# Layer 2 attention: position sums in 128x32 column tiles, and one score tile in three squared on ScalarE

## The chip, the cores and the metric

The kernel runs on one core of a Trainium2 chip. A core has engines that run side by side, each with a queue of its own: TensorE (PE in the profile, its weight loads PEld), VectorE (DVE), ScalarE (ACT), GpSimd (POOL) and SyncE (SP, which only issues DMAs here). They tell each other through semaphores when a tile is ready or free. Matmul results go to PSUM[...]; all other tiles lie in SBUF. The metric is the device time of one execution in microseconds, the median of the runs.

## The reference

The whole computation is a four-layer network over x of shape (2, 64, 64, 128) in fp32. Only the attention of layer 2 is touched. There the input is layer-normed, taken as 2 batches of L = 4096 tokens of 128 channels with 4 heads of 32, and this is computed:

```
q, k, v = silu(x @ Wq + bq), silu(x @ Wk + bk), silu(x @ Wv + bv)
u = x @ Wu + bu
rel = pos_w[S - 1 + m - n]                     # a Toeplitz matrix; a table index too large is held at the end
pos_attn = einsum('nm,bmd->bnd', rel, v)
scores = (qh @ kh) / sqrt(32)                  # per head
scores = where(m <= n, scores * scores, 0)
self_attn = silu(scores) @ vh
a = layernorm(concat(self_attn, pos_attn)) * ln_gamma + ln_beta
out = relu(u * a @ Wf + bf) + x
```

So every score is multiplied by a scale, squared, masked causally and put through SiLU before it weighs the values; there is no softmax. The position part is a product of a table of lags with the values, independent of the scores.

## The kernel before

The stages run one after another (layer 0, layer 1, layer 2's attention and FFN, layer 3's). A second copy of the program follows behind a condition and is not executed with these inputs. `layer2_attn` works on blocks of 512 queries: 16 blocks (b, qb), in the order qb = 7, 0, 6, 1, 5, 2, 4, 3 for each batch. A block loops over its 4qb + 4 key chunks of 128, the last four of which are on the diagonal and get narrower (512, 384, 256, 128 queries). 288 chunks are worked in all. For each chunk, `scores(i, k)` computes two PSUM tiles `l2sc` of 128x1024, each with two heads (L1273: four matmuls with 32 rows of contraction, on four row groups of the array). PSUM holds two such tiles, so the next chunk's tile can only be written when the tile of the same place has been read.

The two tiles are then taken out of PSUM and squared into SBUF tiles `l2es` (seven of them), in two different ways. The first tile of each chunk is squared by ScalarE in one instruction, with the scale in it (L1282); on the diagonal VectorE then multiplies its first 128 columns by the causal mask (L1295). The second tile is scaled by VectorE (L1290, and on the diagonal L1286 for the masked 128 columns) and then squared in SBUF by GpSimd (L1297). `silu()` applies SiLU on ScalarE to both tiles of the chunk before (L1303), and `values()` multiplies those of two chunks before with the values, four matmuls of 128x32 weights into four partition groups of one PSUM bank `l2av` (L1316).

Beside this run the jobs of a hand-written planner: generators that issue a piece of their work at each `yield`. After each chunk, as many pieces are taken from the head of the list as the sum of all pieces divided by the chunks left. The jobs are the keys and values of a group of tokens (`keys`), their suffix sums (`suffixes`), the queries of the next block (`prepare`), the position sums (`positions`), and, when a block's chunks are done, `join` (transposition, layer norm, three POOL products L1217 to L1219) and `output` (projection and addition to x). `join` finishes the rest of its block's position sums at once.

`positions` sums the Toeplitz products of a block of 512 queries. The table `toe` holds for each lag d = 0 to 31 a 128x128 block. For each of the four query chunks n of a block, one matmul for each k up to n adds `toe` block n - k times value chunk k (L1178: 128x128 weights, 128 columns moving); all later keys have one and the same table entry, so one product of a suffix sum with the matrix `late` adds them (L1189). The sums of four chunks lie in one PSUM bank `l2pos`, which VectorE copies out (L1199).

The order on each engine's queue is not that of the code: a scheduler sets it when the program is built. For an even stretch of the loop it is, on ScalarE, the square of a chunk, the SiLU of its first tile, the SiLU of its second tile (which waits for GpSimd), then the next chunk; on TensorE the scores of chunk k, the values of chunk k - 2, and a piece of the position sums.

Of the kernel before, what the change touches and what calls it, by code (L numbers as in the profile page):

```python
# [9 lines left out]
AF = mybir.ActivationFunctionType  # L10
ALU = mybir.AluOpType
# [3 lines left out]
P = 128  # L15
# [3 lines left out]
NC = L // P  # L19
# [19 lines left out]
class Net:  # L39
# [928 lines left out]
    def layer2_attn(self):  # L968
# [3 lines left out]
        nc, tc, ins = self.nc, self.tc, self.ins  # L972
        pos_w = ins["L2_attn_pos_rev"]
        with ExitStack() as st:
# [7 lines left out]
                out=flip,  # L982
# [7 lines left out]
            toe = wp.tile([P, L], F32, tag="toe", name="toe")  # L990
            with tc.tile_pool(name="l2r", bufs=1) as rp:
                rev = rp.tile([P, L], F32, tag="rev", name="rev")
                nc.sync.dma_start(
                    out=rev,
# [51 lines left out]
            def finish(key):  # L1046
                while key in jobs:
                    piece(key)
# [120 lines left out]
            def positions(b, qb, i):  # L1169
                finish(("suf", b))  # L1170
                v, suf = vs[b], sufs[b]
                pos = ps.tile([P, 4, C], F32, tag="pos", name=f"l2pos{b}_{qb}", bufs=1)
                done = 0
                for j in range(4):
                    n = 4 * qb + j
                    last = n == NC - 1
                    for k in range(n + 1):
                        nc.tensor.matmul(  # L1178
                            pos[:, j, :],
                            lhsT=toe[:, (n - k) * P : (n - k + 1) * P],  # L1180
                            rhs=v[:, k, :],
                            start=(k == 0),
                            stop=(last and k == n),
                        )
                        done += 1
                        if done % 4 == 0:
                            yield
                    if not last:
                        nc.tensor.matmul(  # L1189
                            pos[:, j, :],  # L1190
                            lhsT=suf[:, 0, n + 1 : n + 2].broadcast_to([P, P]),
                            rhs=late,
                            start=False,
                            stop=True,
                        )
                if i >= 2:
                    finish(("out", i - 2))
                cats[i] = ap.tile([P, 4, 2 * C], F32, tag="cat", name=f"l2a{b}_{qb}")
                nc.vector.tensor_copy(cats[i][:, :, C:], pos)  # L1199
# [52 lines left out]

            root = float(HD) ** -0.5
            raw, squared = [], []

            def scores(i, k):


                b, qb = order[i]
                finish(("keys", b, k // 4))  # L1260
                q, kT = queries[i][0], kTs[b]

                off = max(0, k - 4 * qb) * P
                diag = k >= 4 * qb
                mask = tri.unsqueeze(1).broadcast_to([P, 2, P])
                out = []
                for pair in range(2):
                    t = f"{b}_{qb}_{k}_{pair}"
                    sc = ps.tile([P, 2, 512], F32, tag="sc", name=f"l2sc{t}")
                    for h2 in range(2):  # L1270
                        h = 2 * pair + h2
                        hs = slice(h * HD, (h + 1) * HD)
                        nc.tensor.matmul(  # L1273
                            sc[:, h2, off:],
                            lhsT=kT[hs, k * P : (k + 1) * P],
                            rhs=q[hs, off:],
                            start=True,
                            stop=True,
                        )
                    out.append((sc, ap.tile([P, 2, 512], F32, tag="es", name=f"l2es{t}", bufs=7)))  # L1280
                (sc, es), (sc1, es1) = out
                nc.scalar.activation(es[:, :, off:], sc[:, :, off:], AF.Square, scale=root)  # L1282
                lo = off
                if diag:
                    lo = off + P
                    nc.vector.scalar_tensor_tensor(  # L1286
                        es1[:, :, off:lo], sc1[:, :, off:lo], root, mask, ALU.mult, ALU.mult
                    )
                if lo < 512:
                    nc.vector.tensor_scalar(  # L1290
                        es1[:, :, lo:], sc1[:, :, lo:], root, None, ALU.mult
                    )
                if diag:
                    part = es[:, :, off:lo]
                    nc.vector.tensor_tensor(part, part, mask, ALU.mult)  # L1295
                part = es1[:, :, off:]
                nc.gpsimd.tensor_tensor(part, part, part, ALU.mult)  # L1297
                raw.append((i, k, off, (es, es1)))

            def silu():  # L1300
                i, k, off, es = raw.pop(0)
# [544 lines left out]
```

## Time and profile before

| What | Value |
|---|---|
| Median of 3 runs | 5194.89 us (5192.98 to 5206.92) |
| The profiled execution's own time | 5199.35 us |
| Its span | 5197.4 us |
| Granted TensorE clock, mean | 0.898 |
| Layer 2's attention loop | from about 2150 to 3490 us of the span |
| Position sums L1178, TensorE | 2112 records, mean 293 ns; weight loads mean 199 ns |
| Squares on ScalarE, L1282 | 288, mean 937 ns |
| Evacuations on VectorE, L1290 | 272, mean 1127 ns |
| Squares on GpSimd, L1297 | 288, mean 1751 ns |
| SiLU on ScalarE, L1303 | 576, mean 984 ns |

A matmul in fp32 leaves two records in the trace, so 2112 records are 1056 products. The means mix the wide tiles with the narrow ones of the diagonal. Matmuls on different row or column groups run at the same time, so the time that counts is from the start of one group to the start of the next, not the duration of one record. A line of the waits names who was idle, what released it, the total, how many times, and the longest. The chain of waits is followed back from the last instruction, at each step to whatever released it.

### The profile page before, as it was taken

The numbers are of one execution on the slowest core, as the hardware profiler recorded it, in microseconds if no ns is written. First come the engines' busy times: TensorE is split into PE (matmuls) and PEld (weight loads), VectorE is DVE, ScalarE is ACT, GpSimd is POOL, SyncE is SP. The second block draws the span as 40 slices with busy tenths as digits, with TensorE's granted clock in tenths as the row PEclk, the third lists the DMA queues.
The fourth block names the chain that finished last, engine by engine and source line by source line (L and its number), as shares of the span: only waits on it lengthen the run. The fifth ranks groups of instructions, "written<-read, shape, count | busy, mean of one in ns | idle before, by whom it ended". The sixth has DMA issues, their size and how long they took to land.

```text
span 5197.4 us, 69148 instructions
## 1 busy us (share of the span) xinstructions
PE 4641.6 (89%) x28133; PEld 2278.3 (44%) x28133; DVE 2851.6 (55%) x4850; ACT 2406.8 (46%) x2783; POOL 749.9 (14%) x434
## 2 busy tenths in 40 slices
PE   7999999999999946789889988885999999999776
PEld 6433333443333335444344434443986444444432
DVE  2568776667878888744444344444023333333477
ACT  3556666566666624466666766551003222222200
POOL 1000000000000030244444455440002000000000
PEclk7899999999999968889999999886559999999889
DMA  4222323333233200000000000002320000000000
GB/s 126 65 56 45 60 65 76 84 66 67 51 57 60 44 8 1 24 1 1 1 1 1 1 1 1 1 1 67 122 74 1 0 0 1 0 0 0 5 11 23
DMA packets 132256, 165.10 MB, mean 32 GB/s; under 512 B 13233, under 2 KB 75665, under 8 KB 131025
## 3 DMA queue, kind: packets, MB, share of 16 engines
q1 hardware_dynamic: 110016, 143.38, 12.9%
q10 hardware_dynamic: 21904, 17.12, 1.1%
q8 instruction: 226, 3.70, 0.3%
q14 instruction: 110, 0.89, 0.1%
HBM read 131.10 MB, written 29.36 MB: 31 GB/s over the span
## 4 chain that ended last, share of the span: by engine, by line
PE 73%; DVE 13%; ACT 6%; POOL 5%; issue 2%; DMA 1%; ACTq 0%; DVEq 0%; POOLq 0%; SPq 0%
PE l0sc L593 17%; PE l0o L547 9%; PE scl L1610 8%; PE oTl L1627 8%; PE l2sc L1273 5%; POOL l2es L1297 3%; PE l2pos L1178 3%; PE f3ex L1784 2%; PE l2av L1316 2%; PE f2po L1488 2%; PE f2ph L1462 2%; ACT l2es L1303 2%; DVE l2es L1290 2%; DVE l0acc L615 2%; ACT l2es L1282 2%
## 5 line engine op out<-in xcount | busy, mean ns | idle before, releaser
L615 DVE TENSOR_TENSOR l0acc<-l0acc,l0es 128x1024 f32<-128x1024 f32 x988 | 1209.9, 1225 | 535.6 <-PE l0o L547 370.4
L607 ACT ACTIVATE l0es<-l0sc 128x1024 f32<-128x1024 f32 x992 | 940.3, 1031 | 384.2 <-PE l0sc L593 383.2
L593 PE MATMUL l0sc<-l0mv,ka 64*64 64x512 f32 x8192 | 990.9, 616 | 18.8 <-ACT l0es L607 16.5
L1303 ACT ACTIVATE l2es<-l2es 128x1024 f32<-128x1024 f32 (+3 forms) x576 | 563.5, 984 | 344.0 <-POOL l2es L1297 304.6
L1297 POOL TENSOR_TENSOR l2es<-l2es 128x1024 f32<-128x1024 f32 (+3 forms) x288 | 504.1, 1751 | 671.9 <-DVE l2es L1290 617.5
L1635 DVE TENSOR_TENSOR accl<-accl,esl 128x1024 f32<-128x1024 f32 x240 | 294.1, 1225 | 540.7 <-ACT esl L1621 482.9
L593 PEld LDWEIGHTS l0sc<-l0mv,ka 64*64 64x64 f32 x8192 | 297.6, 136 | 622.8 <-issue 377.2
L1273 PE MATMUL l2sc<-l2q,l2kT 32*128 32x512 f32 (+3 forms) x2304 | 427.6, 642 | 129.6 <-ACT l2es L1282 99.2
L1290 DVE TENSOR_SCALAR l2es<-l2sc 128x1024 f32<-128x1024 f32 (+3 forms) x272 | 306.6, 1127 | 397.9 <-PE l2sc L1273 397.2
L1621 ACT ACTIVATE esl<-scl 128x1024 f32<-128x1024 f32 x240 | 245.5, 1023 | 550.8 <-PE scl L1610 550.8
L547 PE MATMUL l0o<-l0es,l0v 128*32 128x512 f32 x3968 | 495.0, 602 | 0.0
L1610 PE MATMUL scl<-l3qT,l3kT 128*128 128x512 f32 x1024 | 484.0, 595 | 1.8 <-DVE bok_l L247 1.8
L1627 PE MATMUL oTl<-esl,l3v 128*128 128x512 f32 x960 | 448.5, 592 | 0.0
L1178 PEld LDWEIGHTS l2pos<-l2v,toe 128*128 128x128 f32 x2112 | 266.9, 199 | 166.3 <-issue 165.1
L1316 PE MATMUL l2av<-l2es,l2v 128*32 128x512 f32 (+3 forms) x2304 | 317.2, 619 | 2.5 <-ACT l2es L1303 2.5
L1178 PE MATMUL l2pos<-l2v,toe 128*128 128x128 f32 x2112 | 309.3, 293 | 0.0
L1282 ACT ACTIVATE l2es<-l2sc 128x1024 f32<-128x1024 f32 (+3 forms) x288 | 270.0, 937 | 73.0 <-PE l2sc L1273 72.1
L1610 PEld LDWEIGHTS scl<-l3qT,l3kT 128*128 128x128 f32 x1024 | 192.8, 191 | 233.2 <-issue 218.6
L868 POOL TENSOR_TENSOR l1y<-l1y,l1gb 128x1024 f32<-128x1024 f32 x8 | 20.2, 2529 | 1858.5 <-DVE l1y L862 1838.3
L1627 PEld LDWEIGHTS oTl<-esl,l3v 128*128 128x128 f32 x960 | 182.4, 190 | 229.6 <-issue 225.8
L547 PEld LDWEIGHTS l0o<-l0es,l0v 128*32 128x32 f32 x3968 | 106.9, 109 | 337.8 <-issue 337.8
L1273 PEld LDWEIGHTS l2sc<-l2q,l2kT 32*128 32x128 f32 x2304 | 128.0, 195 | 245.9 <-ACT l2es L1282 136.5
(435 smaller groups left out, 4483.0 us busy)
## 6 DMA issues: line engine op xcount, KB each, us to landing
l0mv<-l0qd SPq DMA_DIRECT2D x128, 256.0 KB, 5.8
l0mv<-l0hd SPq DMA_DIRECT2D x256, 128.0 KB, 4.0
l0mv<-l0wd SPq DMA_DIRECT2D x128, 128.0 KB, 6.1
l0wd<-l0rw SPq DMA_DIRECT2D x4, 2048.0 KB, 7.5
l0hd<-l0hst SPq DMA_DIRECT2D x32, 256.0 KB, 2.2
f2w<-in_L_ffn_weight_dram ACTq DMA_DIRECT2D x32, 256.0 KB, 4.2
f2w<-in_L_ffn_weight_dram ACTq DMA_DIRECT2D x8, 1024.0 KB, 4.8
f2w<-in_L_ffn_weight_dram SPq DMA_DIRECT2D x8, 1024.0 KB, 5.1
```

The costliest lines, as they stand in the source:

```text
L547: nc.tensor.matmul(o[0][at : at + HD, :], lhsT=v[:, 2 * j + s, HD * h : HD * (h + 1)], rhs=es[s][:, h, :], start=(j == 0), stop=(j == NX * ...
L593: nc.tensor.matmul(sc[64 * c : 64 * c + 64, h, :], lhsT=ka[rows, k0 : k0 + 64], rhs=mv[rows, yb, :], start=True, stop=True,)
L607: nc.scalar.activation(es, sc, AF.Exp)
L615: nc.vector.tensor_tensor(entry[5], entry[5], es, ALU.add)
L1178: nc.tensor.matmul(pos[:, j, :], lhsT=toe[:, (n - k) * P : (n - k + 1) * P], rhs=v[:, k, :], start=(k == 0), stop=(last and k == n),)
L1273: nc.tensor.matmul(sc[:, h2, off:], lhsT=kT[hs, k * P : (k + 1) * P], rhs=q[hs, off:], start=True, stop=True,)
L1290: nc.vector.tensor_scalar(es1[:, :, lo:], sc1[:, :, lo:], root, None, ALU.mult)
L1297: nc.gpsimd.tensor_tensor(part, part, part, ALU.mult)
L1303: nc.scalar.activation(e[:, :, off:], e[:, :, off:], AF.Silu)
L1316: nc.tensor.matmul(avs[i][hs, off:], lhsT=vs[b][:, k, hs], rhs=es[h // 2][:, h % 2, off:], start=(k == 0), stop=last,)
L1610: nc.tensor.matmul(sc[:, i, :], lhsT=kT[:, k * P : (k + 1) * P], rhs=qs, start=True, stop=True,)
L1627: nc.tensor.matmul(oT, lhsT=v[:, k, :], rhs=es[:, i, :], start=(k == 0), stop=(k == NC - 1),)
```

## The change

Two things are altered, both in layer 2's attention. `positions` now runs over lags d: for each lag it multiplies the table block with all value chunks that it meets in this block of queries, up to four chunks or 512 columns moving at once. The weights are cut in four parts of 128x32 that write four partition groups of the same bank; the suffix products are cut in the same way. A piece of the job is one lag (the lags at the end go together). `scores` no longer has a fixed way for each of the two tiles: a counter runs over all tiles of the stage, and every third tile is squared on ScalarE, the two others go through VectorE and GpSimd. So of three chunks, one has both tiles on VectorE and GpSimd, one has its first tile on ScalarE and one its second. The number of jobs' pieces given to the planner, the buffers and the DMAs stay as they are. In the changed kernel the position matmul is at L1177, the ScalarE square at L1289, the mask product at L1292, the VectorE evacuation at L1301, the GpSimd square at L1304, SiLU at L1310 and the values at L1323.

```diff
--- before.py
+++ after.py
@@ -1170,29 +1170,32 @@
                 finish(("suf", b))
                 v, suf = vs[b], sufs[b]
                 pos = ps.tile([P, 4, C], F32, tag="pos", name=f"l2pos{b}_{qb}", bufs=1)
-                done = 0
+                n0 = 4 * qb
+                for d in range(n0 + 4):
+                    j0 = max(0, d - n0)
+                    for c in range(0, P, 32):
+                        nc.tensor.matmul(
+                            pos[c : c + 32, j0:, :],
+                            lhsT=toe[:, d * P + c : d * P + c + 32],
+                            rhs=v[:, n0 + j0 - d : n0 + 4 - d, :],
+                            start=(d == 0),
+                            stop=False,
+                        )
+                    if d < n0 or j0 == 1:
+                        yield
                 for j in range(4):
-                    n = 4 * qb + j
-                    last = n == NC - 1
-                    for k in range(n + 1):
+                    n = n0 + j
+                    if n == NC - 1:
+                        continue
+                    for c in range(0, P, 32):
                         nc.tensor.matmul(
-                            pos[:, j, :],
-                            lhsT=toe[:, (n - k) * P : (n - k + 1) * P],
-                            rhs=v[:, k, :],
-                            start=(k == 0),
-                            stop=(last and k == n),
-                        )
-                        done += 1
-                        if done % 4 == 0:
-                            yield
-                    if not last:
-                        nc.tensor.matmul(
-                            pos[:, j, :],
-                            lhsT=suf[:, 0, n + 1 : n + 2].broadcast_to([P, P]),
+                            pos[c : c + 32, j, :],
+                            lhsT=suf[:, 0, n + 1 : n + 2].broadcast_to([P, 32]),
                             rhs=late,
                             start=False,
-                            stop=True,
-                        )
+                            stop=(n == min(n0 + 3, NC - 2)),
+                        )
+                yield
                 if i >= 2:
                     finish(("out", i - 2))
                 cats[i] = ap.tile([P, 4, 2 * C], F32, tag="cat", name=f"l2a{b}_{qb}")
@@ -1252,6 +1255,7 @@
 
             root = float(HD) ** -0.5
             raw, squared = [], []
+            turn = [0]
 
             def scores(i, k):
 
@@ -1278,24 +1282,27 @@
                             stop=True,
                         )
                     out.append((sc, ap.tile([P, 2, 512], F32, tag="es", name=f"l2es{t}", bufs=7)))
-                (sc, es), (sc1, es1) = out
-                nc.scalar.activation(es[:, :, off:], sc[:, :, off:], AF.Square, scale=root)
-                lo = off
-                if diag:
-                    lo = off + P
-                    nc.vector.scalar_tensor_tensor(
-                        es1[:, :, off:lo], sc1[:, :, off:lo], root, mask, ALU.mult, ALU.mult
-                    )
-                if lo < 512:
-                    nc.vector.tensor_scalar(
-                        es1[:, :, lo:], sc1[:, :, lo:], root, None, ALU.mult
-                    )
-                if diag:
-                    part = es[:, :, off:lo]
-                    nc.vector.tensor_tensor(part, part, mask, ALU.mult)
-                part = es1[:, :, off:]
-                nc.gpsimd.tensor_tensor(part, part, part, ALU.mult)
-                raw.append((i, k, off, (es, es1)))
+                for sc, es in out:
+                    turn[0] += 1
+                    part = es[:, :, off:]
+                    if turn[0] % 3 == 0:
+                        nc.scalar.activation(part, sc[:, :, off:], AF.Square, scale=root)
+                        if diag:
+                            part = es[:, :, off : off + P]
+                            nc.vector.tensor_tensor(part, part, mask, ALU.mult)
+                        continue
+                    lo = off
+                    if diag:
+                        lo = off + P
+                        nc.vector.scalar_tensor_tensor(
+                            es[:, :, off:lo], sc[:, :, off:lo], root, mask, ALU.mult, ALU.mult
+                        )
+                    if lo < 512:
+                        nc.vector.tensor_scalar(
+                            es[:, :, lo:], sc[:, :, lo:], root, None, ALU.mult
+                        )
+                    nc.gpsimd.tensor_tensor(part, part, part, ALU.mult)
+                raw.append((i, k, off, [es for _, es in out]))
 
             def silu():
                 i, k, off, es = raw.pop(0)
```

## The prediction

> **What bounds the kernel now.** I read the page first, then a table of windows to find the stage, the waits inside it, the chain of waits, and a timeline of an even stretch. The page's span is 5197.4 us. The edit touches one stage, layer 2's attention, and a wholly hidden or wholly exposed edit there can only move these 1340 us (columns after the window: length, then busy time and count of PE, weight loads, DVE, ACT, POOL, then the granted clock):
>
> ```profile
> 2150.00:3490.00 1340.00, 1190.18 (x7806) 585.02 (x7807) 606.33 (x996) 881.18 (x956) 629.54 (x349) 0.92 0.00 1
> 2560.00:2590.00 30.00, 29.50 (x228) 13.38 (x220) 10.96 (x9) 27.60 (x28) 17.03 (x9) 1.00 0.00 1
> ```
>
> TensorE looks full (89%), ScalarE has 66% and POOL 47%. In the even stretch ScalarE is at 92% too, so two engines are nearly full, and shares alone do not say which work to move. The waits of the stage (total us, times, longest):
>
> ```profile
> ACT l2es L1303 <- POOL l2es L1297: 304.6, 199, 8.6
> DVE l2es L1295 <- ACT l2es L1282: 185.5, 59, 8.3
> PE l2sc L1273 <- ACT l2es L1282: 99.2, 89, 7.9
> ```
>
> Each waits on the next: TensorE's scores wait for the ScalarE square that frees a score buffer (L1282), that square stands behind a SiLU (L1303), and the SiLU waits for POOL's square (L1297). The chain of waits (start, us, what) shows one full turn in the even stretch and then the first turn on the diagonal:
>
> ```profile
> 2578.30 1.21 PE l2sc L1273 x8
> ...
> 2579.61 1.23 DVE l2es L1290
> ...
> 2580.91 1.90 POOL l2es L1297
> 2582.84 1.06 ACT l2es L1303
> 2583.89 0.92 ACT l2es L1282
> ...
> 2584.86 1.21 PE l2sc L1273 x8
> ...
> 2590.45 0.92 ACT l2es L1282
> ...
> 2591.40 0.42 DVE l2es L1295
> 2591.82 0.33 DVE l2es L1286
> 2592.15 0.88 DVE l2es L1290
> ...
> 2593.19 1.90 POOL l2es L1297
> 2595.11 1.06 ACT l2es L1303
> ```
>
> Scores, evacuation, POOL square, SiLU, ScalarE square, next scores: 2584.86 - 2578.30 = 6.56 us, and two key chunks pass in it, because the scores of chunk k+1 wait for the square of chunk k, which waits for the POOL square of chunk k-1. So 3.28 us for a chunk. TensorE's own work is just under that (start, us, then line and operation):
>
> ```profile
> 2581.47 1.14 PE L1273 MATMUL l2sc<-l2q,l2kT 32*128 32x512 f32 x8
> 2582.54 1.06 PE L1316 MATMUL l2av<-l2es,l2v 128*32 128x512 f32 x8
> 2583.54 1.16 PE L1178 MATMUL l2pos<-l2v,toe 128*128 128x128 f32 x8
> ...
> 815.77 1.92 PE L547 MATMUL l0o<-l0es,l0v 128*32 128x512 f32 x16
> 817.63 1.12 PE L379 MATMUL l0pk<-l0xT,wqkv 128*128 128x512 f32 x2
> ```
>
> From start to start: scores 1.07, values 1.00, position sums 1.09 (from the 2580.37 group to 2581.47), together 3.16. The last two rows, from layer 0, are 128x32 column tiles, twice as many as a values group: 817.63 - 815.77 = 1.86 us, so a second group in the same tiling costs 0.86 and the first 1.00.
>
> Taking the start of every eighth score matmul in the timelines as a chunk's start, I sorted the 288 chunks: 114 even ones off the diagonal (374.2 us, 3.28 each), 23 of 3.7 to 4.4 us (93.5 us, two position pieces each, TensorE full), 64 diagonal ones (295.0 us), and 87 at the block changes, where output projection, layer norm and left-over position sums run (568.5 us).
>
> **What the Trainium skill says.** PSUM — Partial Sum Buffer, "Engine vs sequencer instructions": the queues of ScalarE, VectorE and GpSimd are strict FIFO, so a waiting instruction holds all behind it. The trace agrees: DVE stood 185.5 us at the mask product (L1295) while L1286 and L1290 behind it had their scores. TensorEngine Tiling (Array Packing), "Key Properties": tiles work in parallel and a change of tiling mode drains the array; agreed, 0.86 against 1.00 us above. GPSIMD Engine Reference, "3.1": a two-input fp32 operation takes about twice VectorE's time; here POOL's 128x1024 square takes 1892 ns, VectorE's evacuation 1223 ns. TensorE: Matmul & The Clock Gate, Part 1: an idle window of about 3.4 us halves the clock; agreed at 2537.03, where after 7.88 us of idling the score group took 2.09 us instead of 1.14.
>
> **The change, part by part.**
>
> *Position sums.* 2112 matmul records of 128x128 (1056 products, two records each) become 2304 of 128x32 by up to 512 columns, the form and shapes of L1316. Four value chunks took 1.09 us alone and 0.92 in a run (28 records and 2 of the suffix from 2463.63 to 2467.08: 0.115 each); now 0.86, since they stand right behind the values group in the same tiling. TensorE gains 0.23 us a chunk where pieces stand alone: even work falls to 1.07 + 1.00 + 0.86 = 2.93. If the tiling switch were still paid, 1.00; if weight loads showed, bounded by the 1.09 of before. The gain counts only where TensorE sets the end. At the block changes, runs of up to some 60 records (7 us) stand on the chain; 6% of that is 0.4 us in 16 blocks: -6 us. The suffix products become four column tiles of 128 columns: same columns, no difference counted.
>
> *Squares.* The tiles now go DVE+POOL, DVE+POOL, ScalarE in turn, so three chunks make a round: c (both tiles by DVE and POOL), a (first tile on ScalarE), b (second on ScalarE). ScalarE loses 96 squares of 0.94 us, DVE and POOL gain 96 each of 1.13 and 1.75. Busy time per round stays below TensorE's 8.8: ScalarE 2 x 1.0 + 6 x 1.06 = 8.4, POOL 4 x 1.89 = 7.6, DVE 4.9. What decides is the order. The built program has on ScalarE, in nearly every even stretch:
>
> ```
> SQ a0, silu a0, silu a1(POOL) | SQ b1, silu b0(POOL), silu b1 | silu c0(POOL), silu c1(POOL) | SQ a0 ...
> ```
>
> So the square of a stands behind the SiLU of c's second tile, which has to wait for two POOL squares in line. With the chain's durations and 0 at the start of c's scores: DVE c0 1.31 to 2.54, c1 to 3.76; POOL c0 2.61 to 4.51, c1 to 6.41; SiLU c1 6.44 to 7.50; square a0 to 8.42; scores of b start at 8.46. Scores of a started between, at 2.93 and, its second pair, at 3.8 (c1 evacuated), so their POOL square ends at 8.31 and delays nothing. From b to the next c TensorE needs 2.93, and the square b1 (behind SiLU a1, 10.5) ends at 11.46. A round is 11.5 us, 3.83 a chunk, where before it was 9.84. The same working gives 6.56 for two chunks of before, which the trace shows. 114 x 0.55 = +62 us. Bounds: not below 2.93 a chunk (-40 us), since TensorE has that work; not above both POOL squares and the slow clock in each round, 13.5 us (+140).
>
> In the 23 chunks with two position pieces the round is 8.46 + (1.07 + 1.00 + 2 x 0.86) = 12.25, 4.08 each against 4.07: 0.
>
> *Diagonal.* Before, the mask product stands on DVE ahead of the evacuation and waits for ScalarE's square, so a turn (square, mask, two evacuations, POOL, SiLU) covers one chunk: about 5.4, 4.3 and 3.3 us as the tiles shrink. Twelve undisturbed diagonals took 16.9 us on average. Now each tile is handled in its own turn, and only an a chunk keeps the mask ahead of the evacuation. With the same durations (POOL 1.89, 1.47, 1.05, 0.63 us by width) I get about 13 us for a diagonal that begins with b, 14.5 with c, 15.8 with a; 6, 2 and 4 of the twelve begin so: 14.2 on average, 12 x -2.7 = -32 us. Bounds: 0, and 10 us each (TensorE's work there), -83.
>
> *Block changes.* POOL has two more squares in six chunks (3.8 us) next to the 7.1 us of L1217 to L1219, ScalarE one or two fewer. In the stall from 2525.89 to 2537.03 the built order lets one square in between those three products, but then three squares follow: nearly even. I take +0.9 us in 16 blocks, +14, with -30 and +50 as ends.
>
> Sum: +62 - 32 + 14 - 6 = +38 us on the profiled execution's 5199.35 (span 5197.4), which lies 4.5 above the runs' median of 5194.89; on the median, 5233. No DMA is moved: SP's order is the same instruction for instruction.
>
> **Rivals.** (1) Faster: the mask wait. If diagonals fall to TensorE's work, about 10.5 us, all sixteen give -100 us against the +70 of the other terms, near 5165. It decides once a diagonal saves over 4.4 us. For it: 185.5 us of DVE waiting at L1295. Against: the POOL and SiLU part of the turn stays. (2) No change, 5195: the block changes gain what I count as cost, because ScalarE's squares there (stalls of up to 7.9 us) come sooner. (3) Slower still: the round leaves TensorE idle for 1.75 us in 11.5, and the clock halves; scores and values then add some 2 us a round, 38 rounds, +75, near 5300. Against: TensorE has 8.8 us of work in a round, and 1.75 us is about half of the idle window that the page names. (4) The column tiles do not overlap and the sums take four times as long, hundreds of us; L1316 has the same form and does overlap (2304 records of 619 ns in 317.2 us), under 1%.
>
> **How the numbers follow.** Forecast 0.58, with 5212 to 5275 as its own range; (1) 0.19; (2) 0.13; (3) with (4) 0.10. About 0.3%, 15.6 us, is what can be told from no change. Slower 0.58 + 0.10 = 0.68, same 0.13, faster 0.19. The range 5170 to 5300 leaves out half of (1) and half of (3).
>
> **What would show it.** Right: even chunks in rounds of 11.5 us with the step of 8.4 us from c to b; SiLU waiting for POOL well above 304.6 us; DVE's wait at the mask product (now L1292) far below 185.5; position groups 0.86 us behind a values group; other stages unchanged. Wrong: even chunks at 3.28 or less (the order on ScalarE then did not hold), diagonals at 11 us, or a granted clock clearly below 0.92 in the stage.

## The result and the profile after

| | Before | After |
|---|---|---|
| Median (four runs each, same chip) | 5199.78 us | 5238.52 us (5237.44 to 5245.0) |
| Ratio to the kernel before | 1 | 1.0077, 95% interval 1.0058 to 1.0095 |
| The profiled execution's own time | 5199.35 us | 5245.0 us |
| Its span | 5197.4 us | 5242.2 us |
| Mean granted TensorE clock | 0.898 | 0.898 |

The kernel is 0.77% slower, 39 us by the medians. (The four runs before are the three of the table ahead of the prediction and a fourth of 5204.68 us.) The table of windows of the changed kernel, for the stage and for an even stretch (window, length, then busy time and count of PE, weight loads, DVE, ACT, POOL, then the granted clock):

```profile
2150.00:3540.00 1390.00, 1186.92 (x8395) 417.98 (x8394) 725.18 (x1106) 783.27 (x865) 795.43 (x445) 0.92 0.00 1
2570.00:2597.00 27.00, 23.58 (x184) 5.96 (x176) 12.36 (x11) 18.75 (x20) 17.11 (x10) 1.00 0.01 2
```

In the even stretch ScalarE fell from 92% to 69% busy, and TensorE fell with it, from 98% to 87%: the work is spread more evenly over the engines (GpSimd rose from 57% to 63%, VectorE from 37% to 46%), and the two that were nearly full now wait more. The granted clock is 1.00 in this stretch before and after, so nothing here is a slower clock. The groups of the page for the lines of the change (count, then busy time and mean ns of one, then idle time before them and what ended most of it):

```profile
L1310 ACT ACTIVATE l2es<-l2es 128x1024 f32<-128x1024 f32 (+3 forms) x576 | 551.5, 981 | 532.1 <-POOL l2es L1304 518.7
L1304 POOL TENSOR_TENSOR l2es<-l2es 128x1024 f32<-128x1024 f32 (+3 forms) x384 | 670.5, 1762 | 545.1 <-DVE l2es L1301 450.7
L1289 ACT ACTIVATE l2es<-l2sc 128x1024 f32<-128x1024 f32 (+2 forms) x192 | 178.1, 928 | 43.6 <-PE l2sc L1277 43.3
L1177 PE MATMUL l2pos<-l2v,toe 128*32 128x512 f32 (+3 forms) x2304 | 286.0, 587 | 0.0
```

The counts are those of the plan: 384 GpSimd squares and 192 ScalarE squares, 288 of each before. The idle time in the first line, SiLU waiting for GpSimd, is the symptom. The view of waits in the stage (total us, times, longest) sets it beside the others:

```profile
ACT l2es L1310 <- POOL l2es L1304: 518.7, 293, 8.2
PEld l2sc L1277 <- ACT l2es L1289: 204.0, 85, 6.6
DVE l2es L1292 <- ACT l2es L1289: 98.6, 39, 4.7
```

SiLU waited 304.6 us for GpSimd before and waits 518.7 now; VectorE waited 185.5 us at the mask product and waits 98.6. The chain of waits shows one round of three chunks in the even stretch (start, us, what):

```profile
2571.74 1.14 PE l2sc L1277 x8
...
2572.92 1.24 DVE l2es L1301
...
2574.22 3.76 POOL l2es L1304 x2
...
2578.00 1.06 ACT l2es L1310
2579.06 0.92 ACT l2es L1289
...
2580.02 1.14 PE l2sc L1277 x8
2581.16 0.99 PE l2av L1323 x8
2582.16 0.86 PE l2pos L1177 x8
2583.02 1.14 PE l2sc L1277 x8
```

The reader sees both GpSimd squares of a c chunk stand in one line (3.76 us), then the SiLU that waited for them, then the ScalarE square behind that SiLU, and only then the scores of b. From c to b 2580.02 - 2571.74 = 8.28 us, and the round is 2583.02 - 2571.74 = 11.28 us, 3.76 a chunk where it was 3.28. By the timeline, where neighbouring groups overlap and c's scores begin 0.07 us sooner, the starts of the score groups repeat 2.93, 2.93, 5.42.

Sorted into the classes of the prediction (every chunk keeps the class that it had before; us):

| Class | Chunks | Before | After | Difference |
|---|---|---|---|---|
| even, without the three below | 111 | 365.7 | 419.4 | +53.7 |
| seventh chunk of three blocks, 10.8, 10.7 and 10.8 each now | 3 | 8.5 | 32.2 | +23.8 |
| two position pieces | 23 | 93.5 | 94.3 | +0.7 |
| first six chunks of a block, off the diagonal | 80 | 519.3 | 524.3 | +5.0 |
| other long ones | 7 | 49.2 | 46.5 | -2.7 |
| diagonal, blocks with qb of 2 and more | 47 | 201.0 | 179.1 | -22.0 |
| diagonal, short blocks | 16 | 92.2 | 75.9 | -16.3 |

The sum is +42.2 us before rounding. (The last chunk of all is followed by no start and is left out.) The spans differ by 44.8 us.

The three seventh chunks hold a stall at a block change. The first six chunks of the same three blocks are 17 us shorter than before, so most of the +23.8 us is a stall that came later and not a new one; the rows of the first six and the seventh chunks belong together. The timeline of the changed kernel at one of them shows what GpSimd does meanwhile:

```profile
2719.19 2.36 POOL L1221 TENSOR_TENSOR l2a<-l2a,lb 128x1024 f32<-128x1024 f32 x1
2721.62 2.34 POOL L1222 TENSOR_TENSOR l2a<-l2a,l2u 128x1024 f32<-128x1024 f32 x1
2723.92 5.60 POOL L1304 TENSOR_TENSOR l2es<-l2es 128x1024 f32<-128x1024 f32 x3
```

The products of `join` stand ahead of GpSimd's squares here, so SiLU and the ScalarE square behind it come later still.

### The profile page after: what moved, and what is told of

It reads as the page before. It is cut to its first block, busy times and chain, and to the rows that moved or that the text cites. A ratio compares the mean times of both kernels' runs of the same rounds, so it can differ in the third digit from the quotient of the medians.

```text
span 5242.2 us, 70511 instructions
## 1 busy us (share of the span) xinstructions
PE 4631.7 (88%) x28697; PEld 2107.5 (40%) x28697; DVE 2965.1 (57%) x4944; ACT 2305.9 (44%) x2687; POOL 915.9 (17%) x530
## 4 chain that ended last, share of the span: by engine, by line
PE 71%; DVE 14%; POOL 7%; ACT 5%; issue 2%; DMA 1%; SPq 0%; DVEq 0%; ACTq 0%; POOLq 0%
PE l0sc L593 17%; PE l0o L547 8%; PE scl L1617 8%; PE oTl L1634 8%; POOL l2es L1304 5%; PE l2sc L1277 4%; PE f3ex L1791 2%; DVE l2es L1301 2%; PE l2pos L1177 2%; PE f2po L1495 2%; PE f2ph L1469 2%; PE l2av L1323 2%; ACT l2es L1310 2%; DVE l0acc L615 2%; PE l0pw L406 2%
## 5 line engine op out<-in xcount | busy, mean ns | idle before, releaser
L615 DVE TENSOR_TENSOR l0acc<-l0acc,l0es 128x1024 f32<-128x1024 f32 x988 | 1210.0, 1225 | 540.0 <-PE l0o L547 374.2
L1310 ACT ACTIVATE l2es<-l2es 128x1024 f32<-128x1024 f32 (+3 forms) x576 | 551.5, 981 | 532.1 <-POOL l2es L1304 518.7
L1304 POOL TENSOR_TENSOR l2es<-l2es 128x1024 f32<-128x1024 f32 (+3 forms) x384 | 670.5, 1762 | 545.1 <-DVE l2es L1301 450.7
L1301 DVE TENSOR_SCALAR l2es<-l2sc 128x1024 f32<-128x1024 f32 (+3 forms) x366 | 405.8, 1124 | 391.5 <-PE l2sc L1277 381.6
L1277 PE MATMUL l2sc<-l2q,l2kT 32*128 32x512 f32 (+3 forms) x2304 | 450.2, 643 | 178.8 <-ACT l2es L1289 132.3
L1323 PE MATMUL l2av<-l2es,l2v 128*32 128x512 f32 (+3 forms) x2304 | 324.4, 626 | 3.6 <-ACT l2es L1310 3.5
L1177 PE MATMUL l2pos<-l2v,toe 128*32 128x512 f32 (+3 forms) x2304 | 286.0, 587 | 0.0
L1289 ACT ACTIVATE l2es<-l2sc 128x1024 f32<-128x1024 f32 (+2 forms) x192 | 178.1, 928 | 43.6 <-PE l2sc L1277 43.3
L1799 DVE SCALAR_TENSOR_TENSOR x<-f3ex,f3wt,x 128x128 f32<-128x128 f32 x512 | 160.2, 347 | 28.4 <-PE f3ex L1791 19.9
```

Source lines behind the costliest of these rows:

```text
L615: nc.vector.tensor_tensor(entry[5], entry[5], es, ALU.add)
L1177: nc.tensor.matmul(pos[c : c + 32, j0:, :], lhsT=toe[:, d * P + c : d * P + c + 32], rhs=v[:, n0 + j0 - d : n0 + 4 - d, :], start=(d == 0) ...
L1277: nc.tensor.matmul(sc[:, h2, off:], lhsT=kT[hs, k * P : (k + 1) * P], rhs=q[hs, off:], start=True, stop=True,)
L1301: nc.vector.tensor_scalar(es[:, :, lo:], sc[:, :, lo:], root, None, ALU.mult)
L1310: nc.scalar.activation(e[:, :, off:], e[:, :, off:], AF.Silu)
L1323: nc.tensor.matmul(avs[i][hs, off:], lhsT=vs[b][:, k, hs], rhs=es[h // 2][:, h % 2, off:], start=(k == 0), stop=last,)
```

## The experiments

The theory is that of the prediction: off the diagonal a round is as long as the path from c to b, a **latency** through four engines. The rival is the **load**: an engine has more to do than the round holds. Each run was timed several times, against the kernel before on the same chip.

### 1. The two parts apart

First the new `positions` with the old `scores` (the diff is against the changed kernel):

```diff
-                for sc, es in out:
-                    turn[0] += 1
...
+                (sc, es), (sc1, es1) = out
+                nc.scalar.activation(es[:, :, off:], sc[:, :, off:], AF.Square, scale=root)
```

> The position sums of the change with the scores of before. Latency theory (an even chunk is set by the ring scores, VectorE, GpSimd, SiLU, ScalarE square, 6.56 us for two chunks, and TensorE's work lies under it): the even chunks stay at 3.28 us; only the chunks with two position pieces (23 x 0.26 us) and the runs at block changes gain, about -12 us, near 5188. Load theory (TensorE, 89% busy in the stage, is the bound): 0.2 us on each of some 260 position groups, -50 us or more, near 5145.

Measured: 5187.6 us, ratio 0.9982 [0.9973, 0.9992]. The even class (all 114 chunks) took 374.2 us, as before to the tenth, though TensorE has 0.23 us less to do in each chunk. Of the two steps of a turn one fell from 3.16 to 2.94 us and the other rose from 3.40 to 3.61: the turn stays at 6.56. The latency theory's number held. Where the 9 us (by the ratio) were gained is less clear. The chunks with two pieces, where TensorE is full, took 6.0 us less and the larger diagonals 9.0, but the expected gain at the block changes did not come, and all classes together are only 2.7 us below the kernel before in the profiled execution.

The run for the other half was built with both parts by mistake and is a repeat of the changed kernel:

> The scores of the change with the position sums of before. Latency theory: rounds of three even chunks of 8.4 + 3.16 = 11.5 us instead of 9.84, diagonals shorter as in the changed kernel: about +55 us, near 5255, slower than the changed kernel by the 12 to 16 us that the position sums give. Rival (the column tiles are what costs): near 5200 or below.

Measured: 5238.27 us, ratio 1.0088 [1.0074, 1.0102], so it says nothing of the parts; it shows how well the result repeats. The classes of its profile do too: 418.0 us for the 111 even chunks, 32.2 for the three seventh ones and 75.9 for the short diagonals, all within 1.4 us of the table above; but 517.2 for the first six chunks (524.3 there), 53.8 for the other long ones (46.5) and 175.1 for the larger diagonals (179.1). So a difference of 7 us in one class at the block changes, or of 4 us on the larger diagonals, can't be told from none; the three classes of the block changes together repeat, 603.0 and 603.2 us. The half itself, old `positions` and new `scores` (against the kernel before):

```diff
+            turn = [0]
...
-                (sc, es), (sc1, es1) = out
...
+                for sc, es in out:
+                    turn[0] += 1
```

> The new split of the score tiles with the Toeplitz sums of the kernel before (128 columns of weights, one value chunk moving). The run labelled e2_share_only held both parts of the change and is a repeat of the changed kernel. Latency theory (rounds of c, b, a whose length is the path c to b through GpSimd's two squares): GpSimd, VectorE and ScalarE do the same as in the changed kernel, so the even rounds stay near 11.3 us per three chunks; the positions' matmuls are in short pieces again and the block changes and the double-piece chunks lose the 6 to 10 us that the first experiment showed for the new positions: about 5238 + 10 = 5248 us, between 5240 and 5256. Rival, the load on TensorE counts: the old positions cost TensorE more per piece, so the rounds lengthen by about 0.3 us each and the time is above 5260 us.

Measured: 5239.89 us, ratio 1.0078 [1.0063, 1.0092]. The rounds are 3.16, 3.15, 5.19, near 11.5 us in place of 11.28, and the 111 even chunks took 428.9 us in place of 419.4. The whole loss comes with the split of the tiles, and the new position sums take nothing measurable from it.

### 2. Half of one GpSimd square, on the path and off it

In both kernels one 128x1024 GpSimd square in three chunks is cut to 256 of 512 columns of each head, off the diagonal; the other columns stay unsquared. GpSimd is spared nearly the same work, 78 half squares in the first and 76 in the second. In the first it is the second tile of c, on the path; in the second the second tile of a, beside it. The diff is that of the first kernel against the changed one; the second has 4 in place of 2.

```diff
+                    if not diag and turn[0] % 6 == 2:
+                        part = es[:, :, :256]
                     nc.gpsimd.tensor_tensor(part, part, part, ALU.mult)
```

> The changed kernel, but in chunks whose both tiles go through GpSimd (off the diagonal) the GpSimd square of the second tile covers only 256 of 512 columns of each head; that part of the squares is left out. GpSimd loses some 75 x 0.85 us of work. Latency theory: that square is on the ring, so each even round shortens by 0.85 us, 11.3 to 10.4, 38 rounds, and some block changes too: -32 to -45 us, near 5200. Load theory (GpSimd and VectorE simply have more to do): the same as e4_half_a.

> The changed kernel, but in chunks whose first tile goes to ScalarE (off the diagonal) the GpSimd square of the second tile covers only 256 of 512 columns of each head; that part of the squares is left out. GpSimd loses the same 75 x 0.85 us of work as in e3_half_c. Latency theory: this square ends at 8.3 us of the round where 9.4 are enough, so nothing follows from it: 0 to -8 us, near 5236, rounds still 11.3 us. Load theory: the same gain as e3_half_c.

Measured: 5195.18 us, ratio 0.9997 [0.9989, 1.0005], against 5234.54 us, ratio 1.0077 [1.0064, 1.0090]. Against the changed kernel's 5238.5, the same saving is worth 43 us in the one place and 4, within the interval, in the other. In the 111 even chunks it is 32.7 us and 1.9. The chain of waits of the first kernel:

```profile
2562.61 1.14 PE l2sc L1277 x8
...
2565.09 1.90 POOL l2es L1306
...
2567.02 2.06 ACT l2es L1312 x2
2569.07 0.92 ACT l2es L1289
...
2570.04 1.14 PE l2sc L1277 x8
```

From c to b it is now 7.43 us, 0.85 less than 8.28. About 0.95 of GpSimd's time went; the last tenth is not gained because the path changes engines: the SiLU of c's first tile (two SiLUs in a row, 2.06) is now late. The starts repeat 2.93, 2.93, 4.57. In the second kernel they are 2.93, 2.93, 5.42 as in the changed one. GpSimd's load as such does not set the round: the load theory has fallen.

### 3. The order on ScalarE

No work is added or taken away: the SiLUs of a chunk are queued behind the square of the next chunk's tile (against the changed kernel).

```diff
+                        square[0] = (k, nc.scalar.activation(part, ..., AF.Square, scale=root).ins)
...
+                    if square[0][0] == k + 1:
+                        with tc.issue_after(square[0][1]):
+                            nc.scalar.activation(e[:, :, off:], e[:, :, off:], AF.Silu)
```

> The changed kernel with one change of order on ScalarE: the SiLUs of a chunk are queued behind the square of the next chunk's tile instead of ahead of it. No instruction is added or taken away. Latency theory: the long step c to b (score 1.3, VectorE 1.2, GpSimd 3.8, SiLU 1.06, square 0.92) loses the SiLU and the wait for GpSimd ahead of the square, since the square of b's tile no longer stands behind the SiLUs that wait for GpSimd; the round falls from 11.3 to about 9.6 us, which TensorE's 3 x 3.0 us nearly fills: 38 rounds x 1.6 = 60 us less, about 5175 us, between 5160 and 5200. Rival, the load on ScalarE and GpSimd sets the round: nothing changes, 5239 us. Second rival, the late SiLUs make the values late by as much as the scores gain: 5220 to 5240 us.

Measured: 5107.14 us, ratio 0.9822 [0.9809, 0.9836]: 132 us less than the changed kernel, twice what was expected. The waits of this kernel (L1312 is a SiLU queued behind a square; L1314 is one of the chunk before c, since c has no square on ScalarE):

```profile
ACT l2es L1312 <- POOL l2es L1304: 63.6, 34, 4.8
ACT l2es L1314 <- POOL l2es L1304: 59.5, 66, 6.4
```

SiLU's 518.7 us of waiting for GpSimd are 123.1. The round came out near the expected 9.6 us, 2.93 + 3.17 + 3.39 = 9.49, and the 111 even chunks took 66.1 us less, where 60 were expected. The rest of the gain was not in the expectation: the larger diagonals fell from 179.1 to 139.3 us, the first six chunks of the blocks from 524.3 to 502.2 and the three seventh chunks from 32.2 to 22.2. The likely reason is that squares stood behind waiting SiLUs there as well; it was not tested apart.

What keeps the round at 9.49, over TensorE's 3 x 2.93 = 8.79? Two groups of the timeline (start, us, engine and line, operation; in brackets the idle time before it and its releaser):

```profile
2401.19 2.36 DVE L1301 TENSOR_SCALAR l2es<-l2sc 128x1024 f32<-128x1024 f32 x2 [1.70 <-PE l2sc L1277]
2403.12 1.61 PE L1277 MATMUL l2sc<-l2q,l2kT 32*128 32x512 f32 x8
```

VectorE takes both tiles of a c chunk out one after the other, 2.36 us, to 2403.55, and the next scores, begun at 2403.12, last 1.61 us in place of 1.14, because their second tile finds its place still occupied. Two tiles in a row on one engine come with the split of one in three itself. The other 0.24 us lie in a group of values that waits for its SiLU (1.31 us in place of 1.06). A later place for the values was tried on top, with an eighth `l2es` buffer paid for by one buffer of `xT` and one of `selfT`:

```diff
-                    if squared[1:]:
+                    if squared[2:]:
```

> As the run before it, and the values of a chunk are taken one chunk later on TensorE (three chunks behind the scores instead of two), with an eighth buffer for the squared scores; one buffer less for the transposed block and for the block's self-attention sum pays for it. Latency theory: the values' wait for the SiLUs, which the moved SiLUs make longer, is then covered, and the round is what TensorE and ScalarE need, 8.9 us: about 20 to 30 us below the run before it, near 5150 us. Rival, the values were not waiting: the same as the run before it within 5 us. Loss theory: the buffer taken from the transposed blocks stalls the block changes, more than 10 us above the run before it.

Measured: 5099.2 us, ratio 0.9805 [0.9792, 0.9819], 8 us less, not 20 to 30, and the intervals of the two overlap. In the larger blocks the even starts are now 2.93, 2.93, 3.64, again 9.50. All that is over 8.79 now lies in the one score group behind VectorE's pair:

```profile
2395.72 2.36 DVE L1301 TENSOR_SCALAR l2es<-l2sc 128x1024 f32<-128x1024 f32 x2 [1.70 <-PE l2sc L1277]
2397.39 1.86 PE L1277 MATMUL l2sc<-l2q,l2kT 32*128 32x512 f32 x8
```

VectorE ends at 2398.08, and the scores last 0.72 us longer than 1.14. So the values were not what filled the round; the trace points to the pair, which no run took away by itself.

### 4. The mask on the diagonal

The kernel before with the mask product behind VectorE's evacuations:

```diff
+                    evict = nc.vector.tensor_scalar(
...
+                    with tc.issue_after(evict.ins):
+                        nc.vector.tensor_tensor(part, part, mask, ALU.mult)
```

> The kernel before with its diagonal mask on the squared tile moved behind VectorE's evacuations of the other tile (the scheduler had put the mask, which waits for ScalarE's square, ahead of them); nothing else is changed and no tile changes its engine. If the diagonals' gain in the changed kernel comes from this stall of the evacuation behind the mask, the diagonals fall here as well: 16 blocks by 1.5 to 3 us, 25 to 48 us in all, 5150 to 5172 us. Rival, the diagonals gained from the new positions or from the new split of the tiles over the engines: 5190 to 5200 us.

Measured: 5129.6 us, ratio 0.9866 [0.9850, 0.9882], 70 us less than before. The two waits to look at:

```profile
DVE l2es L1296 <- ACT l2es L1282: 54.5, 52, 3.5
ACT l2es L1304 <- POOL l2es L1298: 223.8, 151, 8.6
```

The mask still waits 54.5 us, but no evacuation of its own chunk stands behind it. The larger diagonals took 151.3 us in place of 201.0, the short blocks' 79.8 in place of 92.2, and the even class 374.9, unchanged. So the place of one short instruction, with all else as it was, cost this kernel 62 us on the diagonals. The changed kernel's diagonals are 38 us shorter than before; there two chunks in three evacuate their masked tile ahead of any mask product, but an a chunk still has it in front. This cost is not one of the mask alone: the last run of section 5 leaves it in front and shortens the diagonals by 68 us, because ScalarE's square, for which it waits, comes sooner.

### 5. What the split itself is worth

The old split (first tile of each chunk on ScalarE) with the new position sums, the SiLUs behind the next square as in section 3, and the mask last as in section 4. Next to it the same with the values a chunk later, by the edit of section 3. Against the changed kernel (the lines of the two orders that sections 3 and 4 show are left out):

```diff
-                for sc, es in out:
-                    turn[0] += 1
...
+                square[0] = (k, nc.scalar.activation(es[:, :, off:], sc[:, :, off:], AF.Square, scale=root).ins)
```

> The kernel before with the new Toeplitz sums, with the first tile of every chunk squared on ScalarE as before, with the SiLUs of a chunk queued behind the square of the next chunk, and with the diagonal mask behind VectorE's evacuations: the changed kernel's position part and the two orders, without its split of one tile in three. If it is the order of ScalarE's queue alone that made the fifth run fast, the even chunks fall from 3.28 us to what ScalarE has to do for a chunk, 0.92 + 2 x 1.06 + small gaps = 3.1 us (TensorE: 2.93), which is 20 us less on 114 chunks; with 50 to 65 us from the diagonals and 10 from the positions this gives about 5095 us, between 5075 and 5115, at or below the kernel with one tile in three and the same order (5107). Rival, the split of one in three is what makes that order pay, because ScalarE is the bound with one in two: even chunks stay at 3.28 us, 5120 us or more.

> As the run before it, with the values one chunk later, an eighth buffer for the squared scores and one buffer less for the transposed block and for the self-attention sum. With one in three the same edit gave 5099 against 5107 us. Here ScalarE sets the even chunks at 3.1 us either way, so the gain is in the block changes alone: 0 to 20 us below the run before it. Rival, values were waiting for SiLUs in every chunk of the run before it: more than 25 us below it.

Measured: 5035.94 us, ratio 0.9696 [0.9676, 0.9716], and 5019.8 us, ratio 0.9655 [0.9636, 0.9674], the fastest of all. The first is 66 us by the ratios below one tile in three with the same order on ScalarE (part of that may be the mask's place: its larger diagonals are 11 us shorter and its short ones 4; but of the 64 us between the two profiles 48 lie off the diagonal). Its chain of waits in an even stretch:

```profile
2398.47 1.07 PE l2sc L1277 x8
2399.54 1.00 PE l2av L1325 x8
2400.54 0.86 PE l2pos L1177 x8
2401.40 1.07 PE l2sc L1277 x8
```

The chain has only TensorE in it, here 2.93 us from scores to scores; over the stretch the starts are 3.05 and 2.93 apart in turn. The longer step has values of 1.12 us in place of 1.00. ScalarE is 97% busy there and costs no more than that, as this kernel's table of windows shows (columns as above):

```profile
2390.00:2402.00 12.00, 12.00 (x104) 3.61 (x96) 4.90 (x4) 11.69 (x13) 7.62 (x5) 1.00 0.01 1
```

With the values later it is 2.93 in each chunk of that stretch. Taking squares away from ScalarE, the change's premise, was not needed to reach TensorE's limit.

Last, one edit alone: the kernel before with the SiLUs behind the next square, all else as it was.

```diff
+                        with tc.issue_after(square[0][1]):
+                            nc.scalar.activation(e[:, :, off:], e[:, :, off:], AF.Silu)
```

> The kernel before with one edit: the SiLUs of a chunk queued on ScalarE behind the square of the next chunk. Positions, split of the tiles and the order on VectorE (the mask ahead of the evacuations) stay as before. Latency theory: even chunks fall from 3.28 to about 3.1 us (20 us on 114 chunks; the old position groups cost TensorE 1.1 us in the place of 0.86, so TensorE and ScalarE are both near 3.1); on the diagonals the mask waits for a square that no longer stands behind SiLUs, so part of the 62 us that the mask's place costs there goes too, 30 to 60 us; block changes 10 to 35 us less. Sum: 5195 - 20 - 45 - 20 = about 5110, between 5080 and 5140. Rival, the order pays only together with the mask's new place or the new positions: above 5150.

Measured: 5074.62 us, ratio 0.9762 [0.9746, 0.9779], 124 us less than before, and below the expected range. The chain of waits:

```profile
2402.62 1.09 PE l2pos L1178 x8
2403.71 1.07 PE l2sc L1274 x8
2404.78 0.99 PE l2av L1321 x8
2405.77 1.09 PE l2pos L1178 x8
```

TensorE is full here too, at 1.09 + 1.07 + 0.99 = 3.15 us a chunk; the 0.23 us of the old position groups is now on the path. But the even class gives only 4.8 us of the gain, 369.4 in place of 374.2. Most of it lies elsewhere: the larger diagonals fell from 201.0 to 145.0 us, the short ones from 92.2 to 79.9, and the first six chunks of the blocks from 519.3 to 472.0, where the expectation had 30 to 60 less for the diagonals and 10 to 35 for the block changes. VectorE's wait at the mask product, still ahead of the evacuations here, fell from 185.5 to 100.6 us.

### 6. Column tiles or wide weights

The changed kernel with one 128x128 weight tile for the four column tiles:

```diff
-                    for c in range(0, P, 32):
-                        nc.tensor.matmul(
-                            pos[c : c + 32, j0:, :],
-                            lhsT=toe[:, d * P + c : d * P + c + 32],
...
+                    nc.tensor.matmul(
+                        pos[:, j0:, :],
+                        lhsT=toe[:, d * P : (d + 1) * P],
```

> The changed kernel with one 128x128 weight tile for each table chunk in the place of the four 128x32 column tiles; four value chunks still move per table chunk, 512 columns. A group in column tiles took 0.86 us behind a group of values. Prediction: a wide matmul of 512 columns takes about as long by itself, but it changes TensorE's tiling between the values and the scores, 0.1 us each way, so a group takes about 1.0 us; the rounds are set by the path through GpSimd, not by TensorE, so the kernel stays within 8 us of the changed one, 5239 us, with the double-piece chunks 0.2 us each longer. Rival, column tiles are what makes the group short (a wide matmul takes 1.1 us or more, as the group of four wide matmuls did in the kernel before): 5245 to 5260 us. Second rival, the wide one is shorter: below 5230 us.

Measured: 5244.75 us, ratio 1.0089 [1.0070, 1.0108], not to be told from the changed kernel's 1.0077. Its chain of waits has the group in it:

```profile
2393.22 1.00 PE l2av L1321 x8
2394.22 1.06 PE l2pos L1176 x2
2395.28 1.14 PE l2sc L1275 x8
```

1.06 us in place of 0.86, and near the 1.09 of four matmuls of 128 columns: behind a group of values it is the column tiles that shorten the group. Since four value chunks took 0.92 us in a run of such matmuls (the prediction's working), most of the 0.20 us probably lies in the change of tiling and not in the shape; no run here separates the two. The chunks with two pieces took 98.3 us in place of 94.3, and the rounds 3.12 + 3.12 + 5.23 = 11.47. Of the 0.38 us that the two short steps lose, the long one gives back half.

## Why the prediction was right, and where it was off

- **Even chunks.** Right in mechanism and nearly in size. The round was put at 11.5 us and is 11.28, the step from c to b at 8.46 and is 8.28. The term of +62 us on 114 chunks measured +53.7 on 111; the other three became block changes. Section 2 shows that it is this path and not the load, section 3 that the order on ScalarE makes it.
- **Two position pieces.** 4.08 us each was predicted; 94.3 / 23 = 4.10 was measured.
- **Diagonals.** Right in sign, mis-sized in two ways. Predicted by the kind of chunk that begins them: 13 us (b), 14.5 (c), 15.8 (a); eleven complete ones measured 13.6, 15.9 and 17.3 on average. So the twelve gave -22.0 where -32 was written. The likely reason is that the hand order had too little waiting at the mask product that an a chunk still keeps in front; it was not measured apart. The four short diagonals were counted at nothing and gave -16.3. Together -38.
- **Block changes.** Mis-sized: +14 was taken from a range of -30 to +50; +5.0 in the first six chunks, +23.8 in three seventh chunks and -2.7 in the other long ones make +26, and their sum repeats. In the seventh chunks a score tile waits for a ScalarE square behind a SiLU behind GpSimd, the same path again, with GpSimd's square behind the products of `join`, which the prediction counted as "nearly even" at such a stall.
- **Position sums.** The group is 0.86 us, as predicted from layer 0's rows. Their -6 us at the block changes is not visible as such; alone they gave 9 us, 6 of it in the chunks with two pieces.
- **The sum.** +38 was predicted, +42 measured in the stage. That it is so near is partly luck: the even chunks and the diagonals came out 15 us lower than written, the block changes (with the position sums there) 18 us higher.
- **The rivals.** That the relief at the mask decides (5165) named a real cost. Section 4 prices it at 62 us on the diagonals, but the change takes away 38. The gain at the block changes that was to make up for the rest (5195) turned out a loss of 26 us. Column tiles overlap: 2304 records of 587 ns took 286.0 us. The halved clock did not come in the even stretches, which ran at 1.00. Of some 2.5 us a round that TensorE loses there the longest pause in one piece is 1.71 us, where the prediction had 1.75:

```profile
2580.02 1.14 PE L1277 MATMUL l2sc<-l2q,l2kT 32*128 32x512 f32 x8 [1.71 <-ACT l2es L1289]
```

- **A ratio that was not used.** The factor of about two that the prediction quotes for GpSimd against VectorE does not fit the durations that stand beside it: 1892 to 1223 ns is 1.55, of two different operations. The sums rest on the measured durations.

What the prediction did not see is larger than what it did. It took the order on ScalarE as given. It named the square that "stands behind a SiLU (L1303)" and quoted the Trainium skill (PSUM — Partial Sum Buffer, "Engine vs sequencer instructions") on strict FIFO queues, but used both only for what the change does. The last run of section 5 shows that this place in the queue was 124 us of the time before. Little of it lay in the ring of 6.56 us from which the prediction started, where TensorE's 3.15 us a chunk were close below: some 5 us came from the even chunks, 68 from the diagonals and 47 from the first six chunks of the blocks, by the profiles.

Left open: how much the mask's place is worth once ScalarE's order is mended was not measured alone, and neither was the price of the two smaller sets of buffers (`xT` and `selfT`) that pay for the eighth `l2es`. What VectorE's pair of tiles costs in section 3 was read from the trace and not tested.

## What to carry to other kernels

When a ring of waits passes through several engines, its length depends not only on how long each instruction takes but also on what stands in front of it in its queue. First ask whether the instruction that frees a buffer (here a square out of PSUM) stands behind one that waits for another engine, and swap them, before moving work between engines. Sparing a nearly full engine by a slower one that lies in series can lengthen the ring, as it did here (3.28 to 3.76 us a chunk), though the busy shares look more even; and a gain on a full engine counts only after the ring is shorter than that engine's work. Look at block changes and diagonals too: here most of what the order was worth in the kernel before lay there and not in the even stretch.

## What the runs showed of the hardware

The same 512 columns against the same 128x128 block of the table cost 1.06 us as one wide fp32 matmul between values and scores, and 0.86 us as four 128x32 column tiles behind a group of values in that tiling, although each of the four tiles moves all 512 columns: their records overlap (of 2304 such records, 587 ns each on average, the whole takes 286.0 us).

A longer stall shows in the clock where the round's short one does not. The changed kernel's chain of waits at one of the three seventh chunks:

```profile
2721.04 1.08 PE l2sc L1277 x4
...
2727.87 2.08 PE l2sc L1277 x4
2729.95 1.86 PE l2av L1323 x8
```

The table of windows has for the stretch after the stall (columns as above):

```profile
2728.00:2735.00 7.00, 7.00 (x28) 1.29 (x28) 2.22 (x2) 4.35 (x5) 3.42 (x2) 0.50 0.01 2
```

TensorE's scores end at 2722.12 (2721.04 + 1.08) and it stands for 5.75 us. After that a score tile took 2.08 us in place of 1.08 and the values 1.86 in place of 1.00, at a granted clock of 0.50. In the even rounds, where the longest pause is 1.71 us, the values after it took 0.99 at a clock of 1.00. Where between the two the limit lies, no run shows.
